# One scan over two states in a selective-scan kernel, its first step made apart

## The chip, the core and the metric

The kernel runs on one core of a Trainium2 chip. The metric is the device time of one execution in microseconds. The engines are named as in the profile: PE (TensorE, matmuls), DVE (VectorE), ACT (ScalarE), POOL (GpSimd) and SP (SyncE, which issues the DMAs). Each engine executes its own instructions in order, and waits where an instruction needs what another engine has not finished.

## What is computed

The input is 8192 rows of 512 numbers. A selective state-space block is followed by a quantized feed-forward block, each inside a layer norm, a modulation and a residual. The change concerns only the recurrence of the first block:

```
delta   = softplus(dlt @ W_dt.T + b_dt)              # [8192, 1024]
A       = -exp(A_log)                                # [1024, 16]
deltaA  = exp(delta[..., None] * A)                  # decay of each step
deltaBx = delta[..., None] * Bm[:, :, None, :] * xc[..., None]

def step(h, inp):                                    # over the 8192 steps
    dA, dBx, c = inp
    h = dA * h + dBx
    return h, einsum("bdn,bn->bd", h, c)
```

Each of the 1024 channels has 16 states `h`; a step multiplies each by its decay and adds an input, and the output of a channel is the sum of its states weighted by `c`.

## The kernel before

**Tiling.** The time axis is cut into 16 chunks of T = 512 steps, and the 1024 channels into ND = 8 blocks of 128, which lie on the partitions. Blocks are taken in NH = 4 parts `h` of DH = 2 blocks (`i`), and the 16 states in NG = 8 groups `g` of GN = 2. One *unit* is two states of one block over one chunk; `slot` numbers the units, 16 for each h and 64 for each chunk, 1024 in all. `where` gives k, h, g, i of a slot.

**One unit** (`unit`, L483) has these parts:

- `db` (L461, POOL) is the input of both states, a tile of 128 x 2 x 512, made two units ahead from the broadcast rows of B and from `du` (L355, POOL), which is delta times xc. There are three `db` buffers.
- `da` (L471, ACT) is the decay, `Exp(delta * na)`, one activation for each of the two states, made one unit ahead. It lies in PSUM, and there are two buffers.
- Two scans (L497, DVE), one for each state, run `h = da * h + db` along the 512 steps. Each starts from a column of `state`, in which the last step of the chunk before was kept.
- The last step of both states is put into `state` (the carry).
- The states are multiplied by the rows of C. PE then transposes the product and adds it up over the states in PSUM (`add_up`, L475, through `add_y`, L388).

Units come in two kinds. In 6 of each 16 (`FAR`, L440) the scan writes into an SBUF tile `hp`, and POOL makes the carry (L512) and the product with C (L513). These are the *far* units. In the other ten, the *near* units, the scan writes over `da`, and DVE makes the product (L521). The carry of a near unit is made by ACT at the beginning of the next unit if that one is far (L494), and by DVE otherwise (L520).

**Order.** The order of each engine's instructions is that of the program text; no planner moves them. Four moments of each unit (BEGIN, MID, GAP, END) are places for the work of other chunks: the norm of the rows, the convolution, the projections, `prep` (delta for one h), `du`, the gate and the output. `TABLE` (L533) gives for each step of each piece the place where it runs, as four times the unit, counted from the chunk's first, plus the moment. `LATER` (L441) gives in the same quarters how long after its unit each product is added up by PE.

`prep` (L343) is two Softplus activations, for the two blocks of one h. [...] a table is loaded before it (L347) and before the next Exp (L471).

`x_proj_out` (L325) copies the projection that holds dlt, B and C for a chunk from PSUM into `dbc` and writes B and C to memory, from which `load_bc` reads them back as broadcast rows.

Of the kernel before, what the change touches and what calls it, by code (L numbers as in the profile page):

```python
# [8 lines left out]
F32 = mybir.dt.float32  # L9
# [7 lines left out]
P = 128  # L17
# [81 lines left out]
def mamba_then_fp4_ffn(  # L99
# [27 lines left out]
    T = 512  # L127
# [16 lines left out]
    nc.gpsimd.memset(eps, EPS)  # L144
    slope0 = glob.tile([P, 1], F32, tag="slope0", name="slope0")
    nc.gpsimd.memset(slope0, -1.72)
    sc = glob.tile([P, NK], F32, tag="silu_c", name="silu_c")

    mo = [dram.tile([T, DM], F32, tag=f"mo_{k}", name=f"mo_{k}") for k in range(NC)]
# [8 lines left out]
    with ExitStack() as ma:  # L158
# [166 lines left out]
        def x_proj_out(k, _=None):  # L325
            pb = pend.pop(("pb", k))
            dbc = s1.tile([RK + 2 * NS, T], F32, tag="dbc", name=f"dbc_{k}")
            nc.scalar.activation(dbc, pb[: RK + 2 * NS, :], AF.Copy)
            bc = scr.tile([2 * NS, T], F32, tag="bc", name=f"bc_{k}")
            nc.sync.dma_start(bc, dbc[RK:, :])  # L330
            dbcs[k], bcd[k] = dbc, bc


        def prep_mm(k, h):
# [8 lines left out]
        def prep(k, h):  # L343
            delta = s2.tile([P, DH, T], F32, tag="delta", name=f"delta_{k}_{h}")
            for i in range(DH):
                d = h * DH + i
                nc.scalar.activation(  # L347
                    delta[:, i, :], pend.pop(("pd", k, d)), AF.Softplus, bias=bdt[:, d : d + 1]
                )
            deltas[k, h] = delta  # L350

        def make_du(k, d):
            h, i = divmod(d, DH)
            du = pools["du"].tile([P, T], F32, tag="du", name=f"du_{k}_{h}_{i}")
            nc.gpsimd.tensor_tensor(du, deltas[k, h][:, i, :], xcs[k, h * DH + i], ALU.mult)  # L355
            dus[k, h, i] = du

        def z_mm(k, m):
# [79 lines left out]


        FAR = (1, 3, 5, 9, 11, 13)  # L440
        LATER = (7, 7, 5, 10, 5, 16, 6, 3, 11, 8, 8, 8, 7, 9, 3, 3)  # L441

        def where(slot):
            k, r = divmod(slot, SLOT_C)
# [13 lines left out]
        def make_db(slot):  # L458
            k, h, g, i = where(slot)
            db = pools["db"].tile([P, GN, T], F32, tag="db", name=f"db_{slot}")  # L460
            nc.gpsimd.tensor_tensor(  # L461
                db, bct[slot // DH, 0], dus[k, h, i].unsqueeze(1).to_broadcast([P, GN, T]), ALU.mult
            )
            pend["db", slot] = db

        def make_da(slot, q):
            k, h, g, i = where(slot)
            d, n = h * DH + i, g * GN + q
            if q == 0:
                pend["da", slot] = pools["da"].tile([P, GN, T], F32, tag="da", name=f"da_{slot}")  # L470
            nc.scalar.activation(  # L471
                pend["da", slot][:, q, :], deltas[k, h][:, i, :], AF.Exp, scale=na[:, d, n : n + 1]
            )
# [9 lines left out]
        def unit(slot):  # L483
            k, h, g, i = where(slot)
            d = h * DH + i

            r = slot % SLOT_S
            far = r in FAR
            db = pend.pop(("db", slot))

            da = hs = pend.pop(("da", slot))
            to = pools["h"].tile([P, GN, T], F32, tag="hp", name=f"hp_{slot}") if far else hs
            if ("carry", slot - 1) in pend:
                nc.scalar.activation(*pend.pop(("carry", slot - 1)), AF.Copy)  # L494
            for q in range(GN):
                n = g * GN + q
                nc.vector.tensor_tensor_scan(  # L497
                    to[:, q, :], da[:, q, :], db[:, q, :], state[:, d, n : n + 1],
                    ALU.mult, ALU.add,
                )  # L500
            if slot + 1 < NSLOT:
                make_da(slot + 1, 0)
            carry = state[:, d, g * GN : (g + 1) * GN]
            run(slot, MID)
            if slot + 1 < NSLOT:
                make_da(slot + 1, 1)
            run(slot, GAP)
            if slot + 2 < NSLOT:
                make_db(slot + 2)
            c_rows = bct[slot // DH, 1]  # L510
            if far:
                nc.gpsimd.tensor_copy(carry, to[:, :, T - 1])  # L512
                nc.gpsimd.tensor_tensor(to, to, c_rows, ALU.mult)  # L513
                add = slot, to
            else:
                hc = pools["h"].tile([P, GN, T], F32, tag="hc", name=f"hc_{slot}")
                if r + 1 in FAR:
                    pend["carry", slot] = carry, hs[:, :, T - 1]
                else:
                    nc.vector.tensor_copy(carry, hs[:, :, T - 1])  # L520
                nc.vector.tensor_tensor(hc, hs, c_rows, ALU.mult)  # L521
                add = slot, hc
            if LATER[r] < 4:
                add_up(*add)
            else:
                at(slot + LATER[r] // 4, LATER[r] % 4, add_up, *add)
            if i == DH - 1:
                del bct[slot // DH, 0], bct[slot // DH, 1]
            run(slot, END)
# [2 lines left out]

        TABLE = {  # L533
            "norm": (
                (-323, -306, -300, -300, -297, -296, -292),
                (-307, -293, -293, -291, -289, -287, -281),
                (-305, -287, -280, -278, -277, -271, -266),
                (-290, -270, -266, -265, -262, -260, -253),
            ),
            "conv": (  # L540
                (-252, -246, -246, -243, -237, -234), (-229, -223, -219, -217, -211, -209),
                (-200, -194, -194, -188, -182, -179), (-171, -166, -166, -162, -156, -154),
                (-143, -137, -134, -133, -127, -126), (-120, -114, -114, -107, -104, -100),
                (-90, -88, -82, -78, -70, -69), (-60, -58, -56, -53, -47, -45),
            ),
            "x_proj": (
                (-36, -34, -31),
            ),
            "prep": (
                (-23, -17), (52, 54), (106, 112), (162, 164),  # L550
            ),
            "du": (
                (-15,), (-10,), (57,), (60,), (119,), (125,), (173,), (190,),
            ),
            "z": (
                (-14, -8, -4), (0, 6, 7), (59, 66, 66), (88, 98, 98), (152, 157, 160),
                (172, 174, 174), (176, 180, 183), (185, 191, 194),
            ),
            "skip": (
                (9, 17), (24, 30), (89, 94), (102, 120), (150, 152), (159, 182), (206, 210),  # L560
                (222, 228),
            ),
            "gate": (
                (67,), (67,), (134,), (134,), (195,), (196,), (259,), (262,),
            ),
            "gate_t": (
                (68, 77), (79, 87), (136, 142), (145, 150), (197, 203), (209, 215), (264, 270),
                (271, 275),
            ),
            "out": (  # L570
                (277, 277, 286), (288, 298, 304), (358, 359, 361), (370, 385, 389),
            ),
        }
        steps = {
            "norm": (load_x, norm_sum, norm_var, norm_rstd, norm_x, norm_t, norm_out),
            "conv": (conv_mm, conv_raw, conv_diag, conv_taps, conv_act, conv_out),
            "x_proj": (x_proj_0, x_proj_1, x_proj_out),
            "prep": (prep_mm, prep),
            "du": (make_du,),
            "z": (z_mm, z_act, z_out),  # L580
            "skip": (skip_act, skip),
# [4 lines left out]
        for k in range(NC):  # L586
            for name, fns in steps.items():
                if k == 0 and name in ("norm", "conv", "x_proj"):
                    continue
                for m, times in enumerate(TABLE[name]):  # L590
                    for fn, time in zip(fns, times):
                        if k == 1 and name == "norm":
                            time -= 4 * (6 if m > 1 else 4)
                        if k == 0 and name == "du" and time < 0:
                            time = min(time, 4 * -3 + GAP)
                        slot, moment = divmod(time, 4)
                        at(k * SLOT_C + slot, moment, fn, k, m)
# [5 lines left out]
        with tc.tile_pool(name="modp", bufs=1, side="right") as mp, tc.tile_pool(  # L603
# [140 lines left out]
            def neg_a():  # L744

                nc.vector.tensor_scalar(cw, cw, 0.5, None, ALU.mult)
                nc.scalar.activation(na, na, AF.Exp)
                nc.vector.tensor_scalar(na, na, -1.0, None, ALU.mult)

            load_x(0, 0)  # L750
            load_wm(0)
# [53 lines left out]
            on(20, x_proj, 0, 0)  # L805
            on(29, x_proj, 0, 1)
            on(29, x_proj_out, 0)
            for n, idx in enumerate((2, 5, 3, 4)):
                h = 8 + 6 * n
                for b in range(2):  # L810
                    on(h - 5 + 3 * b, mod_fetch, idx, b)
                    on(h - 3 + 3 * b, mod_mm, idx, b)
                if idx in (3, 4):
                    on(h + 1, mod_row, idx)
# [209 lines left out]
```

## Time and profile before

| | |
|---|---|
| Median of 3 runs | 5993.54 us (5990.07 to 5995.64) |
| Profiled execution, its own time | 5987.67 us |
| Its span | 5985.9 us |
| DVE busy in the span | 4924.4 us (82%) |
| POOL busy | 4141.6 us (69%) |
| ACT busy | 3080.0 us (51%) |
| PE busy | 5356.8 us (89%) |
| First scan to last scan starts | 157.7 to 3860.5 us |

The span runs from the first to the last instruction of the profiled execution. A busy share over the whole span is a mean over two stages, the scan stage up to about 3860 us and the feed-forward stage after it, in which DVE and POOL are less busy. In the lines of a group the part ahead of the bar is the line of the kernel, the engine, the operation, output and inputs by the program's names, the shapes and the count; after the bar are busy microseconds, the mean nanoseconds of one, and the idle time of the engine just before them with what ended most of it.

### The profile page before, as it was taken

The numbers are of one execution on the slowest core, as the hardware profiler recorded it, in microseconds if no ns is written. First come the engines' busy times: TensorE is split into PE (matmuls) and PEld (weight loads), VectorE is DVE, ScalarE is ACT, GpSimd is POOL, SyncE is SP. The second block draws the span as 40 slices with busy tenths as digits, with TensorE's granted clock in tenths as the row PEclk, the third lists the DMA queues.
The fourth block names the chain that finished last, engine by engine and source line by source line (L and its number), as shares of the span: only waits on it lengthen the run. The fifth ranks groups of instructions, "written<-read, shape, count | busy, mean of one in ns | idle before, by whom it ended". The sixth has DMA issues, their size and how long they took to land.

```text
span 5985.9 us, 60300 instructions
## 1 busy us (share of the span) xinstructions
PE 5356.8 (89%) x20772; PEld 3200.9 (53%) x20772; DVE 4924.4 (82%) x5007; ACT 3080.0 (51%) x5708; POOL 4141.6 (69%) x2415
## 2 busy tenths in 40 slices
PE   7788888889889889889888897679999999999999
PEld 4555565566555555555655655534444444444444
DVE  7999999999999999999999999875666666666654
ACT  6676676766776676766766665422222222222222
POOL 4999999999999999999999999732222222222221
PEclk9989999999999999999999998789999999999999
DMA  5444444444444444444444444410000000000000
GB/s 179 158 151 158 148 155 155 155 153 157 153 155 152 155 156 157 157 154 153 153 156 155 154 151 156 165 37 27 27 23 25 27 27 25 24 26 27 27 23 13
DMA packets 220553, 659.79 MB, mean 110 GB/s; under 512 B 24371, under 2 KB 36787, under 8 KB 220246
## 3 DMA queue, kind: packets, MB, share of 16 engines
q1 hardware_dynamic: 220246, 655.94, 33.7%
q8 instruction: 163, 2.67, 0.2%
q14 instruction: 144, 1.18, 0.1%
HBM read 615.48 MB, written 40.38 MB: 110 GB/s over the span
## 4 chain that ended last, share of the span: by engine, by line
PE 42%; DVE 23%; POOL 17%; ACT 10%; issue 8%; DMA 0%; DVEq 0%; POOLq 0%; SPq 0%; ACTq 0%
DVE da L497 12%; PE pg L945 10%; PE po L962 10%; POOL db L461 10%; PE pu L945 10%; ACT da L471 4%; POOL hp L513 4%; DVE hc L521 3%; DVE hp L497 3%; PE po L423 3%; PE y L392 2%; PE cv L268 2%; PE pz L366 2%; PE pt L913 2%; PE cv L296 1%
## 5 line engine op out<-in xcount | busy, mean ns | idle before, releaser
L461 POOL TENSOR_TENSOR db<-bc,du 128x1024 f32<-128x1024 f32 x1024 | 2395.0, 2361 | 38.2 <-DVE da L497 32.0
L497 DVE TENSOR_TENSOR_SCAN da<-da,state,db 128x512 f32<-128x512 f32 x1280 | 1645.3, 1285 | 85.7 <-ACT da L471 38.6
L471 ACT ACTIVATE da<-delta,na 128x512 f32<-128x512 f32 x2048 | 1407.7, 689 | 428.9 <-DVE hc L521 296.6
L87 POOL TENSOR_TENSOR hq<-xn,sc 128x1408 f32<-128x1408 f32 x64 | 189.2, 2956 | 1319.2 <-DVE xn L82 1319.2
L497 DVE TENSOR_TENSOR_SCAN hp<-da,state,db 128x512 f32<-128x512 f32 x768 | 941.0, 1267 | 44.9 <-ACT state L494 25.5
L392 PE MATMUL y<-ident,hc 128*128 128x128 f32 x5120 | 738.2, 294 | 224.4 <-DVE hc L521 183.6
L513 POOL TENSOR_TENSOR hp<-hp,bc 128x1024 f32<-128x1024 f32 x384 | 905.4, 2358 | 30.7
L392 PEld LDWEIGHTS y<-ident,hc 128*128 128x128 f32 x5120 | 633.3, 151 | 397.4 <-DVE hc L521 245.8
L521 DVE TENSOR_TENSOR hc<-da,bc 128x1024 f32<-128x1024 f32 x640 | 781.6, 1221 | 26.5 <-PE y L392 1.3
L945 PE MATMUL pg<-wg,xqT 128*128 128x512 f32 (+1 forms) x1536 | 653.5, 569 | 44.0 <-ACT xqT L937 44.0
L945 PE MATMUL pu<-wu,xqT 128*128 128x512 f32 (+1 forms) x1536 | 635.9, 557 | 0.0
L962 PE MATMUL po<-wd,hqT 128*128 128x512 f32 x1408 | 616.6, 594 | 0.0
L950 ACT ACTIVATE g<-pg 128x512 f32<-128x512 f32 (+1 forms) x192 | 107.8, 561 | 958.2 <-PE pg L945 958.2
L366 PE MATMUL pz<-w_in,hT 128*128 128x256 f32 x2048 | 483.1, 390 | 33.9 <-DVE z L381 29.1
L268 PE MATMUL cv<-hT,w_in 128*128 128x512 f32 x1024 | 476.9, 609 | 30.3 <-ACT delta L347 14.8
L945 PEld LDWEIGHTS pg<-wg,xqT 128*128 128x128 f32 x1536 | 290.6, 193 | 361.9 <-issue 251.0
L423 PE MATMUL po<-w_o,xc 128*128 128x512 f32 x1024 | 462.0, 600 | 20.3 <-DVE z L381 12.2
L296 PE MATMUL cv<-raw,taps 128*128 128x512 f32 x1024 | 469.0, 601 | 12.5 <-ACT taps L282 12.5
L951 DVE TENSOR_TENSOR h<-g,pu 128x512 f32<-128x512 f32 (+1 forms) x192 | 123.4, 643 | 427.0 <-PE pu L945 422.0
L392 PE MATMUL y<-ident,hp 128*128 128x128 f32 x3072 | 449.0, 295 | 26.9 <-POOL hp L513 26.9
L945 PEld LDWEIGHTS pu<-wu,xqT 128*128 128x128 f32 x1536 | 291.8, 190 | 313.3 <-issue 245.0
L392 PEld LDWEIGHTS y<-ident,hp 128*128 128x128 f32 x3072 | 393.4, 153 | 112.8 <-issue 50.0
(118 smaller groups left out, 6332.2 us busy)
## 6 DMA issues: line engine op xcount, KB each, us to landing
bc<-bc SPq DMA_DIRECT2D x1024, 512.0 KB, 4.5
x<-in_x_dram SPq DMA_DIRECT2D x64, 256.0 KB, 4.7
mo<-po SPq DMA_DIRECT2D x64, 256.0 KB, 2.1
h<-in_x_dram SPq DMA_DIRECT2D x64, 256.0 KB, 2.6
x<-mo SPq DMA_DIRECT2D x64, 256.0 KB, 2.6
out_dram<-x SPq DMA_DIRECT2D x64, 256.0 KB, 2.0
w_in<-in_w_inT_dram SPq DMA_DIRECT2D x2, 2048.0 KB, 9.2
wm<-in_wmod_dram SPq DMA_DIRECT2D x8, 512.0 KB, 4.6
```

The costliest lines, as they stand in the source:

```text
L268: nc.tensor.matmul(ps, lhsT=w_in[:, f, o : o + P], rhs=hT[k][:, f, :], start=(f == 0), stop=(f == NK - 1),)
L296: nc.tensor.matmul(v, lhsT=taps[:, i, :], rhs=raw[:, i : i + T], start=(i == 0), stop=(i == 3))
L366: nc.tensor.matmul(pz[:, b, :], lhsT=hT[k][:, f, t0 : t0 + P], rhs=w_in[:, f, o : o + DH * P], start=(b == 0 and f == 0), stop=(f == NK - ...
L392: nc.tensor.matmul(y[:, j, i * P : (i + 1) * P], lhsT=src[:, j * P : (j + 1) * P], rhs=ident, start=start and j % 2 == 0, stop=stop, is_tr ...
L423: nc.tensor.matmul(pend["po", k, j], lhsT=xcs[k, d][:, j * P : (j + 1) * P], rhs=w_o[:, d, :], start=(d == 0), stop=(d == ND - 1),)
L461: nc.gpsimd.tensor_tensor(db, bct[slot // DH, 0], dus[k, h, i].unsqueeze(1).to_broadcast([P, GN, T]), ALU.mult)
L471: nc.scalar.activation(pend["da", slot][:, q, :], deltas[k, h][:, i, :], AF.Exp, scale=na[:, d, n : n + 1])
L497: nc.vector.tensor_tensor_scan(to[:, q, :], da[:, q, :], db[:, q, :], state[:, d, n : n + 1], ALU.mult, ALU.add,)
L513: nc.gpsimd.tensor_tensor(to, to, c_rows, ALU.mult)
L521: nc.vector.tensor_tensor(hc, hs, c_rows, ALU.mult)
L945: nc.tensor.matmul(ps[:, :w], lhsT=qT[:, k, :], rhs=wt[:, k, o : o + w], start=(k == 0), stop=(k == NK - 1),)
L962: nc.tensor.matmul(po, lhsT=hT[:, f, :], rhs=wd[:, f, :], start=(f == 0), stop=(f == NF - 1))
```

## The change

The two scans of a unit become one scan over 1024 elements, that is, over the two rows of 512 one after the other. So that the second state does not go on from the end of the first, the decay of the first step of each row is made 0. Then the scan needs no start value, and what the first step must give, `exp(delta0 * A) * state + delta0 * B0 * x0`, is put into the first column of `db` instead.

- **Decay 0.** After delta of a block is made, its first column is overwritten with 1e30 (`huge`). `na` is at most -1e-28, so the exponent is -100 or less.
- **First step.** For each block `prep` has four more small activations on ACT: the decay of the first step for 16 states (`e0`), delta0 times xc0, that times B0 (`db0`), and the fill with `huge`. A new step `prep_add` multiplies `e0` by `state` and adds it to `db0`, two small operations on DVE for each block.
- **B0.** The 16 values of B of a chunk's first step are needed on all partitions: a small matmul into the PSUM tile of the projection (`first_mm`) and a copy by ACT (`first_out`), once a chunk.
- **Units.** `db` and `du` leave out their first column. Before the first `da` of each unit, ACT copies two columns of `db0` into the first column of each row of `db`. All near units leave their carry to ACT, so L520 goes.
- **Places.** `LATER` and `TABLE` have other numbers, and `x_proj` and `prep` have places for their new steps.

```diff
@@ x_proj_out and after it
-            dbcs[k], bcd[k] = dbc, bc
+            dbcs[k], bcd[k], pend["pb", k] = dbc, bc, pb
+
+        def first_mm(k, _=None):
+            nc.tensor.matmul(
+                pend["pb", k][:, :NS], lhsT=dbcs[k][:, 0:1].to_broadcast([RK + 2 * NS, P]),
+                rhs=ident[: RK + 2 * NS, RK : RK + NS], start=True, stop=True,
+            )
+
+        def first_out(k, _=None):
+            bf = small.tile([P, NS], F32, tag="bf", name=f"bf_{k}", bufs=1)
+            nc.scalar.activation(bf, pend.pop(("pb", k))[:, :NS], AF.Copy)
+            pend["bf", k] = bf
@@ prep
+                e0 = small.tile([P, NS], F32, tag="e0", name=f"e0_{k}_{d}", bufs=DH)
+                db0 = small.tile([P, NS], F32, tag="db0", name=f"db0_{k}_{d}")
+                pend["e0", k, d], pend["db0", k, d] = e0, db0
+            for i in range(DH):
+                d, d0 = h * DH + i, delta[:, i, 0:1]
+                nc.scalar.activation(pend["e0", k, d], na[:, d, :], AF.Exp, scale=d0)
+                nc.scalar.activation(d0, d0, AF.Copy, scale=xcs[k, d][:, 0:1])
+                nc.scalar.activation(pend["db0", k, d], pend["bf", k], AF.Copy, scale=d0)
+                nc.scalar.activation(d0, huge, AF.Copy)
             deltas[k, h] = delta
+
+        def prep_add(k, h):
+            for d in range(h * DH, (h + 1) * DH):
+                e0, db0 = pend.pop(("e0", k, d)), pend["db0", k, d]
+                nc.vector.tensor_tensor(e0, e0, state[:, d, :], ALU.mult)
+                nc.vector.tensor_tensor(db0, db0, e0, ALU.add)
@@ make_du
-            nc.gpsimd.tensor_tensor(du, deltas[k, h][:, i, :], xcs[k, h * DH + i], ALU.mult)
+            nc.gpsimd.tensor_tensor(
+                du[:, 1:], deltas[k, h][:, i, 1:], xcs[k, h * DH + i][:, 1:], ALU.mult
+            )
@@
-        LATER = (7, 7, 5, 10, 5, 16, 6, 3, 11, 8, 8, 8, 7, 9, 3, 3)
+        LATER = (7, 5, 7, 9, 6, 16, 6, 3, 10, 12, 7, 10, 7, 8, 4, 4)
@@ make_db
-                db, bct[slot // DH, 0], dus[k, h, i].unsqueeze(1).to_broadcast([P, GN, T]), ALU.mult
+                db[:, :, 1:], bct[slot // DH, 0][:, :, 1:],
+                dus[k, h, i][:, 1:].unsqueeze(1).to_broadcast([P, GN, T - 1]), ALU.mult,
@@ make_da, for the first state
+                first = pend["db0", k, d][:, g * GN : (g + 1) * GN]
+                nc.scalar.activation(pend["db", slot][:, :, 0], first, AF.Copy)
@@ unit
-            for q in range(GN):
-                n = g * GN + q
-                nc.vector.tensor_tensor_scan(
-                    to[:, q, :], da[:, q, :], db[:, q, :], state[:, d, n : n + 1],
-                    ALU.mult, ALU.add,
-                )
+            flat = lambda t: t.rearrange("p q t -> p (q t)")
+            nc.vector.tensor_tensor_scan(flat(to), flat(da), flat(db), 0.0, ALU.mult, ALU.add)
...
-                if r + 1 in FAR:
-                    pend["carry", slot] = carry, hs[:, :, T - 1]
-                else:
-                    nc.vector.tensor_copy(carry, hs[:, :, T - 1])
+                pend["carry", slot] = carry, hs[:, :, T - 1]
@@ TABLE: the rows that the text refers to (norm and conv have small shifts)
             "x_proj": (
-                (-36, -34, -31),
+                (-36, -34, -30, -27, -25),
             ),
             "prep": (
-                (-23, -17), (52, 54), (106, 112), (162, 164),
+                (-21, -18, -5), (54, 54, 59), (110, 112, 114), (161, 163, 176),
             ),
             "du": (
-                (-15,), (-10,), (57,), (60,), (119,), (125,), (173,), (190,),
+                (-15,), (-4,), (55,), (61,), (118,), (124,), (164,), (182,),
             ),
@@ neg_a
-                nc.vector.tensor_scalar(na, na, -1.0, None, ALU.mult)
+                nc.vector.tensor_scalar(na, na, -1.0, -1e-28, ALU.mult, ALU.min)
```

## The prediction

> **What bounds the kernel now.** I read the page's strip of busy tenths first: it falls into a scan stage and a feed-forward stage, and the edit touches only the first. Then the busy times over that stage, from the first scan to the last:
>
> ```profile
> core 0: us, PE busy (x) PEld busy (x) DVE busy (x) ACT busy (x) POOL busy (x), PEclk, DMA share, GB/s
> 155.60:3860.50 3704.90, 3227.00 (x14820) 2153.84 (x14821) 3530.59 (x3316) 2470.29 (x4773) 3522.66 (x1974) 0.94 0.47 154
> ```
>
> Columns are stretch, length, then busy time of each engine. DVE and POOL are both busy for 95% of it, ACT for 67%. So DVE work may be cut, but POOL stands 182 us below the stage, and nothing here makes POOL shorter. Next the costliest groups:
>
> ```profile
> L461 POOL TENSOR_TENSOR db<-bc,du 128x1024 f32<-128x1024 f32 x1024 | 2395.0, 2361 | 38.2 <-DVE da L497 32.0
> L497 DVE TENSOR_TENSOR_SCAN da<-da,state,db 128x512 f32<-128x512 f32 x1280 | 1645.3, 1285 | 85.7 <-ACT da L471 38.6 <-POOL state L512 16.3 <-POOL db L461 4.8
> L497 DVE TENSOR_TENSOR_SCAN hp<-da,state,db 128x512 f32<-128x512 f32 x768 | 941.0, 1267 | 44.9 <-ACT state L494 25.5 <-ACT da L471 19.4
> ```
>
> Two facts are in the idle columns: DVE's scans wait little (131 us in all), and part of that is for writes of `state` by POOL (L512) and ACT (L494), which concern columns that the waiting scan doesn't use. Then the DVE timeline, for the pace of a unit (start, duration):
>
> ```profile
> 2042.15 2.61 DVE L497 TENSOR_TENSOR_SCAN da<-da,state,db 128x512 f32<-128x512 f32 x2
> 2044.80 0.16 DVE L520 COPY state<-da 128x2 f32<-128x2 f32 x1
> 2044.87 1.21 DVE L521 TENSOR_TENSOR hc<-da,bc 128x1024 f32<-128x1024 f32 x1
> 2046.01 2.61 DVE L497 TENSOR_TENSOR_SCAN da<-da,state,db 128x512 f32<-128x512 f32 x2
> ...
> 2052.72 2.62 DVE L497 TENSOR_TENSOR_SCAN da<-da,state,db 128x512 f32<-128x512 f32 x2 [0.43 <-POOL state L512]
> 2055.43 1.23 DVE L521 TENSOR_TENSOR hc<-da,bc 128x1024 f32<-128x1024 f32 x1
> 2056.57 2.45 DVE L497 TENSOR_TENSOR_SCAN hp<-da,state,db 128x512 f32<-128x512 f32 x2
> 2058.94 0.66 DVE L306 SCALAR_TENSOR_TENSOR xc<-raw,cv 128x512 f32<-128x512 f32 x1
> ```
>
> A near unit takes 3.86 us from start to start with the carry copy and 3.85 without: that copy is already hidden. A far unit takes 2.37. A chunk has 40 near and 24 far units and 24 other DVE operations at 0.59 a step: 154.2 + 56.9 + 14.2 = 225.3 us. The pattern repeats every 232.1 us (L347's table load at 1419.63 and 1651.72), so DVE idles some 7 us a chunk. DVE sets the pace. Last, the hand-overs after `prep` of unit 13 (ACT) and around unit 60 (DVE, POOL):
>
> ```profile
> 1600.90 1.28 ACT L347 ACT_TABLE_LOAD   x1
> 1602.20 1.27 ACT L347 ACTIVATE delta<-pd,bdt 128x512 f32<-128x512 f32 x2
> 1603.48 1.28 ACT L471 ACT_TABLE_LOAD   x1
> 1604.78 2.75 ACT L471 ACTIVATE da<-delta,na 128x512 f32<-128x512 f32 x4
> ```
> ```profile
> 1606.29 2.62 DVE L497 TENSOR_TENSOR_SCAN da<-da,state,db 128x512 f32<-128x512 f32 x2 [0.85 <-ACT da L471]
> ```
> ```profile
> 1531.56 4.67 POOL L461 TENSOR_TENSOR db<-bc,du 128x1024 f32<-128x1024 f32 x2
> 1539.98 2.37 POOL L461 TENSOR_TENSOR db<-bc,du 128x1024 f32<-128x1024 f32 x1
> 1543.52 2.35 POOL L461 TENSOR_TENSOR db<-bc,du 128x1024 f32<-128x1024 f32 x1
> ```
> ```profile
> 1534.36 2.62 DVE L497 TENSOR_TENSOR_SCAN da<-da,state,db 128x512 f32<-128x512 f32 x2 [0.21 <-issue]
> 1542.38 2.62 DVE L497 TENSOR_TENSOR_SCAN da<-da,state,db 128x512 f32<-128x512 f32 x2 [0.26 <-POOL db L461]
> 1546.85 2.61 DVE L497 TENSOR_TENSOR_SCAN da<-da,state,db 128x512 f32<-128x512 f32 x2
> ```
>
> `prep` holds ACT for 3.88 us (1600.90 to 1604.78). The scan at 1606.29 starts only after the second half of its `da` (two times 0.72 after 1604.78), though its first half needs only the first. With the `state` waits this says that order is kept by whole tiles, not by columns. And POOL is hardly ahead: the scans at 1534.36, 1542.38 and 1546.85 start 0.5, 0.0 and 1.0 us after their `db` (ready at 1533.9, 1542.35, 1545.87).
>
> [...] L244 (one column, pointer scale) measures 291 and the table load 1283[...]. [...]
>
> **Part by part.**
> *The scan.* [...] Near unit 3.59, far 2.25: 40 and 24 of them are 197.6 us against 211.1. Saved: 13.5 us a chunk. [...]
> *`prep_add`.* [...] About 1.8 of it falls in stalls described below; 1.0 counts.
> *Carries.* L520 goes (worth nothing, see above); its 256 copies join ACT at L494's 168 ns, ahead of `da`. The waits of scans on `state` go too: about 42 us in the whole run.
> *ACT in every unit.* The first-column copy, like L289 (195 ns, 0.15 a step), comes before `da`. From the end of `hc` of unit s−1: 0.03, carry 0.20, copy 0.15, two `da` 1.42, hand-over 0.05: `da` of s+1 is ready 1.85 later. A far unit gives it 2.25 less the 0.09 by which scan and `hc` overlap: no stall, 0.3 to spare.
> *ACT in `prep`.* [...] `prep` grows from 3.88 to 5.98 us. Bounds: 1.6 to 2.9 more, −32 to +51 us over 64 `prep`.
> What that does: at unit 13 (far, starting at t), `da` of 14 is ready at t + 1.9, `prep` ends at 7.9, `da` of 15 at 9.5. DVE has done units 13 and 14 at 2.25 + 3.59 = 5.84. Stall: 3.7 us. The same sum with the present numbers gives 0.9, and 0.85 is measured. Walking ACT and DVE through the 64 units so, with the new table: 3.7 at 13, 3.7 at 28, 2.8 at 40, 4.5 at 59 (with a `norm_x` behind it), 2.2 in the dense norm steps of units 53 to 58, 0.5 elsewhere: 17.4.
> Sum for DVE and ACT: 197.6 + 14.2 + 1.0 + 17.4 = 230.2 us a chunk, 1.9 under today.
> *The new wait.* The copy writes a tile that POOL has just filled. If order is kept by tiles, it waits for POOL's `db`, and `da` is queued behind it: a scan then starts at least 1.65 us after its `db`. The trace has leads of 0.0, 0.5, 1.0. In a stretch where POOL never pauses this is one shift, not a loss for each unit; it becomes a loss where POOL waits for a far scan that is now later (L512, 110 us today). Not shown by the trace: nothing to 8 us a chunk; I take 2.8, a good half microsecond for each group of 16 units.
> *At nothing:* POOL's operations one column shorter; the fill of `huge`, `first_mm` and `first_out` (once a chunk); the limit on `na` (once). POOL's cover is the 5% that it idles.
> Sum: 233.0 − 232.1 = +0.9 us, by 16: **+14 us**. Against the profiled execution (5987.67, span 5985.9) that is 6002; the median shown is 5.9 higher, so **6008 us**.
>
> **The rivals.**
> A, faster: the copy doesn't wait for POOL, or POOL keeps its lead. For it: DVE's sum is certain to fall, and POOL catches up in each `prep` stall. Against: the leads above. 16 × (230.2 − 232.1) = −30, and −70 with a cheap scan or `prep`: about 5945. It decides while the copy's waits cost less than 1.1 us a chunk.
> B, faster still: ACT's stalls fall where DVE would wait for POOL anyway, and POOL alone is the bound: 3522.7/16 = 220.2, with 1% of waits 222.4 a chunk, −155: 5838. Against: a stall of 3.7 four times in a chunk exceeds what POOL is behind.
> C, clearly slower: POOL, ACT and DVE in series, at the full 8 us: +100: 6095. It decides from 1.9 us of added waits a chunk.
> D, slower: `db` on rows of 511 from an odd element. POOL operations of 1024 columns differ by pattern (L69 2310, L87 2007 ns); at +300 ns POOL needs 239 a chunk: 6105. It decides from 0.15 us a `db`.
>
> **How the numbers follow.** Forecast 0.42, A 0.24, B 0.08, C 0.18, D 0.08. Its own range is 5975 to 6045. For eight in ten I take in A's and most of C's: 5915 to 6085. About 0.2% (12 us) can be told from no change. Of the forecast's 0.42, 0.05 is faster, 0.14 same and 0.23 slower; A gives 0.22 and 0.02; C and D are slower: faster 0.35, same 0.16, slower 0.49.
>
> **What would show it.** One scan of 128x1024 at 2.33 to 2.35 us; DVE's busy time down by some 170; ACT's up by about 380; DVE's wait for ACT's `da` up from 58 to over 200 us, in lumps near 3.5 at each `prep`; waits for `state` gone from the scans; the first-column copy waiting for POOL's `db`. It is wrong if the lumps are under 2 us (then A), if the copy never waits for POOL (A), if POOL is over 98% busy (B), or if `db` is longer than 2.4 us (D).

## The result, and the profile after

The changed kernel takes 6043.98 us (median of 6 runs, 6023.51 to 6054.97) against 5996.4 us of the kernel before (6 runs beside it). The ratio is 1.0076, 95% interval 1.0058 to 1.0093: slower by some 45 us. The profiled execution took 6043.94 us, its span is 6042.2 us.

Busy time of the engines over the scan stage of the kernel after, in the columns of the same view of before (stretch, length, PE, PEld, DVE, ACT, POOL):

```profile
155.60:3915.00 3759.40, 3258.77 (x14862) 2181.26 (x14863) 3459.31 (x2290) 2718.53 (x6587) 3517.38 (x1973) 0.93 0.47 152
```

DVE has 71 us less to do than before (3459 for 3531), ACT 248 more, POOL 5 less. DVE's idle time in the stage rose from 174 to 300 us (length less busy). So the change did take work from DVE, and more than that came back as waits. First scan to last scan starts 169.3 to 3918.6 us: the stage begins 11.6 us later, and is 46.5 us longer, 2.9 a chunk. Behind it lie 2123.6 us against 2125.4: nothing else changed.

The costliest groups of the page after (busy time and mean of one behind the bar, then idle time before and its releasers):

```profile
L494 POOL TENSOR_TENSOR db<-bc,du 128x1022 f32<-128x1022 f32 x1024 | 2392.8, 2357 | 30.2 <-DVE da L532 26.0
L532 DVE TENSOR_TENSOR_SCAN da<-da,db 128x1024 f32<-128x1024 f32 x640 | 1461.2, 2283 | 71.3 <-ACT da L507 53.8
...
L532 DVE TENSOR_TENSOR_SCAN hp<-da,db 128x1024 f32<-128x1024 f32 x384 | 875.3, 2279 | 89.9 <-ACT da L507 69.0
```

A flat scan takes 2283 and 2279 ns, 1461.2 + 875.3 = 2336.5 us in all against 2586.3 before: 250 us less, and the carry copies of L520, some 40 us, are gone too. But DVE's busy time fell by only 71. The missing 220 us are two groups that the kernel before hadn't got, from the list of DVE's groups:

```profile
L381 DVE TENSOR_TENSOR db<-db,e 128x16 f32<-128x16 f32 x128 | 170.4, 1331 | 11.0 <-ACT db L373 3.6
L380 DVE TENSOR_TENSOR e<-e,state 128x16 f32<-128x16 f32 x128 | 50.1, 391 | 33.7 <-ACT e L371 33.7
```

These are the two operations of `prep_add`, on 16 columns each. One takes 1331 ns on average, more than a product of 1024 columns (1221). Together they are busy for 220.5 us, 13.8 a chunk. The timelines of DVE and of POOL at one `prep_add` show why (start, duration):

```profile
1448.26 0.44 DVE L380 TENSOR_TENSOR e<-e,state 128x16 f32<-128x16 f32 x1 [0.99 <-ACT e L371]
1448.93 2.08 DVE L381 TENSOR_TENSOR db<-db,e 128x16 f32<-128x16 f32 x1 [0.23 <-ACT db L373]
1450.93 0.16 DVE L380 TENSOR_TENSOR e<-e,state 128x16 f32<-128x16 f32 x1
1451.20 1.06 DVE L381 TENSOR_TENSOR db<-db,e 128x16 f32<-128x16 f32 x1
```
```profile
1446.33 2.35 POOL L545 TENSOR_TENSOR hp<-hp,bc 128x1024 f32<-128x1024 f32 x1
1448.63 2.35 POOL L494 TENSOR_TENSOR db<-bc,du 128x1022 f32<-128x1022 f32 x1
1450.94 1.29 POOL L386 TENSOR_TENSOR du<-delta,xc 128x511 f32<-128x511 f32 x1
```

POOL's operations end at 1448.68, 1450.98 and 1452.23. The long DVE operations end at 1448.70, 1451.01 and 1452.26, each 0.02 to 0.03 us later; the only short one (0.16) starts where one POOL operation gives way to the next. The view of waits lists none for POOL at these two lines, only 33.7 and 3.6 us for ACT: the time is inside the instruction. The three long operations here last as long as the rest of what POOL is doing. This is not a choice of examples: of the 256 small operations of the run, 134 took over 300 ns, and every one of them ended 26 to 39 ns after the end of a POOL operation. (Beside POOL's one-column `rstd`, L240, 14 sums were not held: 174 to 176 ns.) The scan stage of the trace before couldn't warn of it. Its products of C (least, median and longest duration 1208/1224/1226 ns), its scans (1253 to 1294) and its convolution (628/672/690) were even throughout; each has one input in PSUM, and so has the gate. The line of the gate's product (the same three numbers), beside a POOL that is busy 95% of the time:

```profile
L404 DVE TENSOR_TENSOR z<-z,y x128: 658/677/687, 217.7 to 3865.8; 128x512 f32<-128x512 f32 x128
```

For L381 after, the same three numbers are 174, 1186 and 2334.

But the feed-forward stage of the trace before did show it. There L81 and L82 are operations of the same kind on the same 512 columns, both with two SBUF inputs, and L82 takes nearly four times as long. The groups of that trace with shapes kept apart, then DVE's and POOL's timeline at one L82:

```profile
L82 DVE SCALAR_TENSOR_TENSOR xn<-e,xn 128x512 f32<-128x512 f32 x66 | 173.5, 2629 | 2.1
L81 DVE SCALAR_TENSOR_TENSOR xn<-e,xn 128x512 f32<-128x512 f32 x66 | 46.9, 711 | 0.4
```
```profile
4524.18 2.96 DVE L82 SCALAR_TENSOR_TENSOR xn<-e,xn 128x512 f32<-128x512 f32 x1
```
```profile
4523.62 2.97 POOL L87 TENSOR_TENSOR hq<-xn,sc 128x1408 f32<-128x1408 f32 x1 [20.43 <-DVE xn L82]
```

L82 ends at 4527.14, 0.55 us after POOL's operation (4526.59). The same holds of all 57 of the 66 that began beside a running POOL operation (545 to 551 ns after its end); the other nine have a median of 691 ns. The distance from POOL's end thus grows with the columns: about 31 ns for 16, 548 for 512, which is some 1.04 ns a column (an estimate from these two medians). So these held operations seem to wait for POOL's end first and to do their own work then.

### The profile page after: what moved, and what is told of

Its sections match the earlier page's. It is cut to its first block, busy times and chain, and to the rows that moved or that the text cites. A ratio compares the mean times of both kernels' runs of the same rounds, so it can differ in the third digit from the quotient of the medians.

```text
span 6042.2 us, 61643 instructions
## 1 busy us (share of the span) xinstructions
PE 5383.5 (89%) x20804; PEld 3226.4 (53%) x20804; DVE 4858.7 (80%) x3983; ACT 3322.2 (55%) x7515; POOL 4136.9 (68%) x2416
## 5 line engine op out<-in xcount | busy, mean ns | idle before, releaser
L494 POOL TENSOR_TENSOR db<-bc,du 128x1022 f32<-128x1022 f32 x1024 | 2392.8, 2357 | 30.2 <-DVE da L532 26.0
L532 DVE TENSOR_TENSOR_SCAN da<-da,db 128x1024 f32<-128x1024 f32 x640 | 1461.2, 2283 | 71.3 <-ACT da L507 53.8
L532 DVE TENSOR_TENSOR_SCAN hp<-da,db 128x1024 f32<-128x1024 f32 x384 | 875.3, 2279 | 89.9 <-ACT da L507 69.0
L425 PE MATMUL y<-ident,hc 128*128 128x128 f32 x5120 | 725.5, 290 | 158.5 <-DVE hc L550 119.3
L550 DVE TENSOR_TENSOR hc<-da,bc 128x1024 f32<-128x1024 f32 x640 | 781.6, 1221 | 77.1 <-PE y L425 39.7
L399 PE MATMUL pz<-w_in,hT 128*128 128x256 f32 x2048 | 503.2, 402 | 39.9 <-ACT delta L361 20.5
L270 PE MATMUL cv<-hT,w_in 128*128 128x512 f32 x1024 | 491.6, 625 | 24.0 <-ACT hT L263 22.3
L298 PE MATMUL cv<-raw,taps 128*128 128x512 f32 x1024 | 481.2, 613 | 10.8 <-ACT taps L284 9.5
L399 PEld LDWEIGHTS pz<-w_in,hT 128*128 128x128 f32 x2048 | 407.1, 204 | 116.8 <-ACT delta L361 29.9
L530 ACT ACTIVATE state<-da 128x2 f32<-128x2 f32 x639 | 108.4, 170 | 649.9 <-DVE hc L550 649.1
```

Source lines behind the costliest of these rows:

```text
L270: nc.tensor.matmul(ps, lhsT=w_in[:, f, o : o + P], rhs=hT[k][:, f, :], start=(f == 0), stop=(f == NK - 1),)
L298: nc.tensor.matmul(v, lhsT=taps[:, i, :], rhs=raw[:, i : i + T], start=(i == 0), stop=(i == 3))
L399: nc.tensor.matmul(pz[:, b, :], lhsT=hT[k][:, f, t0 : t0 + P], rhs=w_in[:, f, o : o + DH * P], start=(b == 0 and f == 0), stop=(f == NK - ...
L425: nc.tensor.matmul(y[:, j, i * P : (i + 1) * P], lhsT=src[:, j * P : (j + 1) * P], rhs=ident, start=start and j % 2 == 0, stop=stop, is_tr ...
L494: nc.gpsimd.tensor_tensor(db[:, :, 1:], bct[slot // DH, 0][:, :, 1:], dus[k, h, i][:, 1:].unsqueeze(1).to_broadcast([P, GN, T - 1]), ALU.mult,
L532: nc.vector.tensor_tensor_scan(flat(to), flat(da), flat(db), 0.0, ALU.mult, ALU.add)
```

## The experiments

Ratios are to the kernel before, run beside each; "after" stands for the changed kernel.

**Without the additions, and with them on POOL.** Two edits of `prep_add`. The first moves both operations to the other engine, the second leaves them out, so the part of the first step that comes from `state` is missing.

```diff
-                nc.vector.tensor_tensor(e0, e0, state[:, d, :], ALU.mult)
-                nc.vector.tensor_tensor(db0, db0, e0, ALU.add)
+                nc.gpsimd.tensor_tensor(e0, e0, state[:, d, :], ALU.mult)
+                nc.gpsimd.tensor_tensor(db0, db0, e0, ALU.add)
```

> The two small adds of prep_add run on POOL in place of DVE. Theory T (a DVE operation with both inputs in SBUF is held until POOL's running operation ends, so that the two take 391 and 1331 ns [...]): DVE's 220 us for them go, POOL takes some 60 us more, and the time falls by 40 to 70 us from 6044, to about before (5985 to 6005). Rival R (the adds lie in the stall that ACT's longer prep makes anyway): within 10 us of 6044.

> prep_add is left out, so the state of the chunk before isn't carried over; everything else stays. Theory T: as with the adds on POOL or a little lower, 5965 to 6000, since POOL has nothing more to do. Rival R: within 10 us of 6044.

Left out: 5914.20 us, ratio 0.9878 (0.9864 to 0.9893), 50 us and more below what was expected. So the other parts of the change make the kernel faster by 1.2%, and the additions alone turn that into a loss. On POOL: 6005.76 us, 1.0031 (1.0020 to 1.0043), at the upper edge of what was expected: better than on DVE and not good. POOL's additions hold up ACT, whose first-column copy needs them (view of waits of that run: who, for whom, us in total, times, longest):

```profile
ACT db L505 <- POOL db L381: 54.4, 31, 3.2
```

The run without additions also shows the stalls after `prep` by themselves. DVE's timeline of one chunk, its scans that waited for ACT:

```profile
1404.15 2.29 DVE L530 TENSOR_TENSOR_SCAN hp<-da,db 128x1024 f32<-128x1024 f32 x1 [3.64 <-ACT state L528]
...
1448.78 2.30 DVE L530 TENSOR_TENSOR_SCAN da<-da,db 128x1024 f32<-128x1024 f32 x1 [2.49 <-ACT da L505]
...
1495.67 2.30 DVE L530 TENSOR_TENSOR_SCAN da<-da,db 128x1024 f32<-128x1024 f32 x1 [0.75 <-ACT da L505]
...
1515.72 2.29 DVE L530 TENSOR_TENSOR_SCAN hp<-da,db 128x1024 f32<-128x1024 f32 x1 [4.51 <-ACT da L505]
...
1579.73 2.30 DVE L530 TENSOR_TENSOR_SCAN da<-da,db 128x1024 f32<-128x1024 f32 x1 [2.31 <-ACT state L528]
```

3.64 + 2.49 + 0.75 + 4.51 + 2.31 = 13.7 us a chunk. Counted by units, the four large ones lie one behind each `prep`: those of units 28, 40 and 59, and that of unit 13 in the next chunk; the 0.75 is at unit 56. Two are listed under ACT's carry (L528), though the flat scan doesn't read `state` at all. ACT's timeline shows what that name is worth. The `da` of the scan at 1404.15 is made here:

```profile
1402.67 1.40 ACT L505 ACTIVATE da<-delta,na 128x512 f32<-128x512 f32 x2
```

It is ready at 1404.07, and the scan starts 0.08 us later. All 83 scans of this run that are listed as waiting for ACT, under either name, start 87 to 103 ns after their own `da`. The name under which a wait is listed needn't be the one that mattered: these are all waits for `da`, 124.7 + 97.5 = 222.2 us. The same holds of the kernel before: 77 of the 78 waits that are listed under `state` there ended 87 to 90 ns after the scan's own `da`.

**What is held: the operation's inputs, or its place.** The changed kernel with a maximum in place of the product, and a copy in place of the sum. The part from `state` is left out here too.

```diff
-                nc.vector.tensor_tensor(e0, e0, state[:, d, :], ALU.mult)
-                nc.vector.tensor_tensor(db0, db0, e0, ALU.add)
+                nc.vector.tensor_reduce(e0[:, 0:1], e0, AX.X, ALU.max)
+                nc.vector.tensor_copy(e0, db0)
```

> The changed kernel with other operations in place of the two additions of a block: a maximum over the 16 columns of e0 (one input in SBUF, output one column) for the product, and a copy of db0 into e0 for the sum. The first step then leaves out the part that comes from the state before. Theory (a VectorE operation with two SBUF inputs is held until GpSimd's running operation ends, one with a single SBUF input is not): the maximum takes under 300 ns on average with its longest under 500, and, if the copy isn't held either, the time is within 15 us of the kernel without the additions (5914). Rival (whatever stands at that place of VectorE is held for GpSimd): both kinds have means of about 400 to 1300 ns and the time stays at 6025 to 6055. Between them: the maximum free and the copy held, 5960 to 6000.

6021.47 us, ratio 1.0061 (1.0046 to 1.0076). DVE's groups of this run, then its timeline at one place and POOL's beside it:

```profile
L381 DVE COPY e<-db 128x16 f32<-128x16 f32 x128 | 174.3, 1362 | 16.4 <-ACT db L373 9.4
L380 DVE TENSOR_REDUCE e<-e 128x1 f32<-128x16 f32 x128 | 20.1, 157 | 34.3 <-ACT e L371 34.3
```
```profile
1436.68 0.17 DVE L380 TENSOR_REDUCE e<-e 128x1 f32<-128x16 f32 x1 [1.24 <-ACT e L371]
1437.34 2.08 DVE L381 COPY e<-db 128x16 f32<-128x16 f32 x1 [0.50 <-ACT db L373]
1439.34 0.16 DVE L380 TENSOR_REDUCE e<-e 128x1 f32<-128x16 f32 x1
1439.60 1.04 DVE L381 COPY e<-db 128x16 f32<-128x16 f32 x1
```
```profile
1434.74 2.35 POOL L545 TENSOR_TENSOR hp<-hp,bc 128x1024 f32<-128x1024 f32 x1
1437.05 2.35 POOL L494 TENSOR_TENSOR db<-bc,du 128x1022 f32<-128x1022 f32 x1
1439.35 1.26 POOL L386 TENSOR_TENSOR du<-delta,xc 128x511 f32<-128x511 f32 x1
```

The maximum at 1436.68 starts and ends in the middle of POOL's operation (1434.74 to 1437.09): it isn't held. The longest of its 128 took 171 ns. The copy from SBUF to SBUF is held to the end of POOL's operation twice (1439.40 and 1440.61), as the sum was. So the place isn't what counts, and "two SBUF inputs" is not all: a plain copy pays too, 1362 ns on average. The rival that everything at this place is held falls. My time for the mixed outcome (5960 to 6000) was too low: it took the two operations as sharing the cost evenly, but the held copy takes up nearly the whole of it (174.3 us against 170.4), and only the 30 us between 50.1 and 20.1 could be won. The run also answers two other rivals. In the changed kernel ACT's first-column copy waits 32.1 us for the sum; here nothing waits for the copy that took its place, and 107 of the 130 us between the kernels with and without additions are still lost. And DVE's own waits for ACT at these two operations aren't the loss: they are 37 us in the changed kernel, 44 here, and 56 in the kernel with paired additions at the same places (below), which is 70 us faster than the changed kernel.

**Fewer operations, and another place.** If a held operation costs the rest of one POOL operation whatever its size, two operations for both blocks of an h should cost half of four. The second of these runs has only that; the first also puts `prep_add` straight behind `prep`.

```diff
-            for d in range(h * DH, (h + 1) * DH):
-                e0, db0 = pend.pop(("e0", k, d)), pend["db0", k, d]
-                nc.vector.tensor_tensor(e0, e0, state[:, d, :], ALU.mult)
-                nc.vector.tensor_tensor(db0, db0, e0, ALU.add)
+            e0, db0 = pend.pop(("both", k, h))
+            nc.vector.tensor_tensor(e0, e0, state[:, h * DH : (h + 1) * DH, :], ALU.mult)
+            nc.vector.tensor_tensor(db0, db0, e0, ALU.add)
@@ the first run only
-                (-21, -18, -5), (54, 54, 59), (110, 112, 114), (161, 163, 176),
+                (-21, -18, -13), (54, 54, 59), (110, 112, 115), (161, 163, 167),
```

> The adds of both blocks of one h in two DVE operations of 32 columns in place of four of 16, and put directly behind prep in all four places, where DVE waits for ACT anyway. Theory T (each add is held by POOL's running operation, whatever its size): half the held time, most of it in the stall: 5930 to 5970, below before. Rival (the cost is in the work or the waits, not in the count): 6000 or more.

> The changed kernel with the additions of both blocks of an h in one product and one sum of 32 columns, at the changed kernel's own places. Theory (a held operation costs what is left of GpSimd's operation, whatever its size, so the count decides): busy time of the additions 110 to 150 us in place of 220, time 5950 to 5990. Rival (it was the earlier place directly behind prep that gained in the run with paired additions): 6010 to 6045.

At the old places: 5973.27 us, ratio 0.9976 (0.9969 to 0.9983); straight behind `prep`: 5931.90 us, 0.9906 (0.9891 to 0.9920). Both are as expected, and both beat the kernel before. DVE's groups of the faster one:

```profile
L383 DVE TENSOR_TENSOR db<-db,e 128x32 f32<-128x32 f32 x64 | 72.9, 1140 | 13.0 <-ACT db L376 8.2
L382 DVE TENSOR_TENSOR e<-e,state 128x32 f32<-128x32 f32 x64 | 63.5, 992 | 53.9 <-ACT e L374 52.8
```

Twice the columns, and the sum's mean is no longer than that of 16 columns. 136.4 us are left of 220.5 (143.5 at the old places), so the count brings some 80 us of busy time and 60 us of time (1.0076 to 0.9976). The place brings another 42 (to 0.9906). In the changed kernel two of the four `prep_add` lie some 6 us after the stall that their `prep` caused, so DVE pays for both. Here are those stalls with their additions in the changed kernel's DVE timeline, and then the same units in the faster run:

```profile
1497.88 2.30 DVE L532 TENSOR_TENSOR_SCAN da<-da,db 128x1024 f32<-128x1024 f32 x1 [2.49 <-ACT da L507]
...
1504.52 2.33 DVE L381 TENSOR_TENSOR db<-db,e 128x16 f32<-128x16 f32 x1
...
1570.86 2.29 DVE L532 TENSOR_TENSOR_SCAN hp<-da,db 128x1024 f32<-128x1024 f32 x1 [4.67 <-ACT da L507]
1576.97 1.21 DVE L380 TENSOR_TENSOR e<-e,state 128x16 f32<-128x16 f32 x1
1578.21 1.19 DVE L381 TENSOR_TENSOR db<-db,e 128x16 f32<-128x16 f32 x1
```
```profile
1457.36 0.85 DVE L382 TENSOR_TENSOR e<-e,state 128x32 f32<-128x32 f32 x1 [0.17 <-ACT e L374]
1458.31 0.19 DVE L383 TENSOR_TENSOR db<-db,e 128x32 f32<-128x32 f32 x1
1459.79 2.30 DVE L534 TENSOR_TENSOR_SCAN da<-da,db 128x1024 f32<-128x1024 f32 x1 [1.28 <-ACT da L509]
...
1528.39 1.16 DVE L382 TENSOR_TENSOR e<-e,state 128x32 f32<-128x32 f32 x1 [1.29 <-ACT e L374]
1529.66 2.21 DVE L383 TENSOR_TENSOR db<-db,e 128x32 f32<-128x32 f32 x1
```

The additions now lie within the wait for `da`: DVE's waits for it fall from 122.8 to 45.1 us (8.8 more are listed under the carry), while those for `e0` at the additions rise from 33.7 to 52.8.

**Two variants of that kernel.**

```diff
@@ the one
-        LATER = (7, 5, 7, 9, 6, 16, 6, 3, 10, 12, 7, 10, 7, 8, 4, 4)
+        LATER = (7, 7, 5, 10, 5, 16, 6, 3, 11, 8, 8, 8, 7, 9, 3, 3)
@@ the other
-            nc.vector.tensor_tensor(e0, e0, state[:, h * DH : (h + 1) * DH, :], ALU.mult)
-            nc.vector.tensor_tensor(db0, db0, e0, ALU.add)
+            nc.gpsimd.tensor_tensor(e0, e0, state[:, h * DH : (h + 1) * DH, :], ALU.mult)
+            nc.gpsimd.tensor_tensor(db0, db0, e0, ALU.add)
```

> The kernel with paired additions behind prep, with the LATER numbers of the kernel before. If the new LATER numbers are worth nothing of themselves: 5925 to 5940, within 0.15% of the paired kernel. If they were needed for the faster units (TensorE adding up too early for POOL's far products or too late for the buffers): 5950 to 6010.

> The paired additions behind prep, on POOL in place of DVE. POOL is not held by itself, but waits for ACT's prep and ACT's next first-column copy waits for POOL, as in the run with single additions on POOL (6006). Theory: POOL's waiting for prep costs more than DVE's being held, so slower than the paired kernel on DVE: 5960 to 6000. Rival (only the holding cost anything): 5890 to 5920.

With the old `LATER`: 5946.93 us, 0.9936 (0.9921 to 0.9951), between the two expectations. The intervals of 0.9906 and 0.9936 just fail to meet, so the new numbers are worth a little, some 0.3%. The other new places of `TABLE` were not tried by themselves. On POOL: 5998.04 us, 1.0020 (1.0012 to 1.0029), as expected of the theory. The additions are short on POOL (32 columns took it 242 to 267 ns), but scans wait 221 us for `da` (130 under that name, 91 under the carry's), as they do without additions, ACT's copy waits 32.5 us for POOL's sum, and in the scan stage DVE waits 69 us for ACT's `z`, against 8 without additions. Here being held, inside a stall that is there anyway, was cheaper than another hand-over between engines.

**The small activations spread out.** The four small activations of a block are moved from `prep` to two later near units, the additions straight behind them, once on DVE and once on POOL. This was meant to break up the stalls.

```diff
-                (-21, -18, -5), (54, 54, 59), (110, 112, 114), (161, 163, 176),
+                (-21, -18, -14, -13, -6, -5), (54, 54, 58, 59, 62, 63),
+                (110, 112, 114, 115, 122, 123), (161, 163, 170, 171, 178, 179),
...
-            "prep": (prep_mm, prep, prep_add),
+            "prep": (prep_mm, prep, first_0, add_0, first_1, add_1),
```

> The four small activations of each block are taken out of prep and put into two later near units, where ACT has 1.6 us to spare, and the adds, still on DVE, right after them. Theory A (the 2.1 us that they add to prep are paid in full by DVE's wait for da): that wait falls from 123 to under 75 us, but the held adds now lie on DVE's path with nothing beside them, so the time moves by -70 to +10 us from 6044. Rival (prep's length is hidden): the wait for da stays over 110 us.

> Both edits together. Theories T and A: the two costs are gone, the time falls by 90 to 150 us from 6044, to 5895 to 5955, below before. Rival P (POOL alone is the bound by then): POOL over 97% busy in the scan stage and the time at 5960 or more.

6135.68 us, 1.0250 (1.0234 to 1.0265), and on POOL 6090.64 us, 1.0173 (1.0158 to 1.0189): both much slower, and both outside their expectations, the second by far. POOL isn't the bound that its rival named: it is busy 3560 of 3792 us of the scan stage (94%). The waits of DVE in the first:

```profile
DVE e L386 <- ACT e L373: 119.0, 48, 12.0
...
DVE da L544 <- ACT da L519: 31.1, 31, 1.5
```

The waits for `da` did fall, from 122.8 to 31 us. But DVE now meets ACT's small activations in the middle of a unit and waits for them, 119 us for 34, and the additions, still held (283 us busy), have no stall to lie in.

**One part alone in the kernel before.** First only the flat scan (no start value, so the second state runs on from the first and no chunk carries in); then only four small activations for each block in `prep`, into tiles that nothing reads.

```diff
-            for q in range(GN):
-                n = g * GN + q
-                nc.vector.tensor_tensor_scan(
-                    to[:, q, :], da[:, q, :], db[:, q, :], state[:, d, n : n + 1],
-                    ALU.mult, ALU.add,
-                )
+            flat = lambda t: t.rearrange("p q t -> p (q t)")
+            nc.vector.tensor_tensor_scan(flat(to), flat(da), flat(db), 0.0, ALU.mult, ALU.add)
@@ the other run: in prep, after both Softplus
+            for i in range(DH):
+                d = h * DH + i
...
+                nc.scalar.activation(e0, na[:, d, :], AF.Exp, scale=delta[:, i, 0:1])
+                nc.scalar.activation(d1, delta[:, i, 0:1], AF.Copy, scale=xcs[k, d][:, 0:1])
+                nc.scalar.activation(db0, e0, AF.Copy, scale=d1)
+                nc.scalar.activation(d1, eps, AF.Copy)
```

> The kernel before with one scan over both states and nothing else of the change, so the second state goes on from the end of the first and no state is carried. This is the gain by itself. Theory: DVE's sum falls from 225.3 to 211.5 us a chunk and POOL's 220 becomes the bound, with 1 to 2% of waits: 130 to 165 us under before, 5820 to 5860. Rival (POOL already sets the pace, the gain is hardly there to be given back): 5940 or more.

> The kernel before with the four small activations of each block added in prep, into tiles that nothing reads, and nothing else. Theory A (2.1 us of ACT in each of 64 prep are paid in full by DVE, 0.4 us of slack apart): 100 to 140 us over before, 6085 to 6125. Rival (ACT, busy for two thirds, hides them): within 20 us of before.

The flat scan alone: 5960.66 us, 0.9954 (0.9937 to 0.9970). The scans are as fast as in the changed kernel (2290 and 2282 ns), and yet only some 28 us come out of 244. The expectation (5820 to 5860) was missed, and the time is the rival's. The rest became waits of DVE, here from that run's list:

```profile
DVE da L496 <- ACT da L471: 156.1, 140, 3.0
DVE hp L496 <- ACT state L494: 65.1, 48, 2.5
DVE da L496 <- POOL db L461: 48.6, 65, 1.6
DVE hc L517 <- PE y L392: 31.3, 14, 3.3
```

Before, they were 38.6, 25.5, 4.8 and 1.3. (The waits under `state` end 86 to 102 ns after the scan's own `da` here too.) With the places as they were, ACT and POOL don't deliver faster than DVE used to ask. The small activations alone: 6113.11 us, 1.0210 (1.0195 to 1.0226). In the old kernel a longer `prep` costs 125 us, as expected.

**Is it still `prep` without the additions?** The changed kernel without the additions and without three of the four small activations; only the fill is kept, and the first step is left out.

```diff
-                nc.scalar.activation(pend["e0", k, d], na[:, d, :], AF.Exp, scale=d0)
-                nc.scalar.activation(d0, d0, AF.Copy, scale=xcs[k, d][:, 0:1])
-                nc.scalar.activation(pend["db0", k, d], pend["bf", k], AF.Copy, scale=d0)
                 nc.scalar.activation(d0, huge, AF.Copy)
```

> The changed kernel without prep_add and with only the fill left of the four small activations; the first step's result is taken from a tile of zeros, so it is left out. To be held against the run without the adds (5914). Theory A: 1.6 us less in each prep, 60 to 100 us under 5914, down to 5815 to 5855, where POOL's sum stops it. Rival: within 20 us of 5914.

5940.65 us, 0.9923 (0.9908 to 0.9938): the expectation was missed by 85 us and more, and it is even slower than with all four (0.9878). What the theory said of `da` came true: with those listed under the carry, DVE's waits for it fell from 222.2 to 158.3 us (124.3 + 34.0). But others grew by more: those of the products with `z`, for ACT and PE, from 59.2 to 118.4 us, and those for POOL's `db` from 9.9 to 39.6. POOL is busy 3512 us of the 3653 from first to last scan (96%). So once the additions are gone, a shorter `prep` only moves the waits to other places. Which order of which engine keeps these two kernels at 5914 and 5941 isn't settled; that POOL stands at 96 to 97% there speaks for POOL being close to its limit, but no run here cut POOL's work.

## Why the prediction was right, step by step

The time lies 36 us above the forecast, within its own range and on its side. It is right as a sum of terms that were off both ways, and that these nearly cancelled was luck. Most of the signs that the prediction named did not come: the scan took 2.28 us and not 2.33, DVE's busy time in the stage fell by 71 us and not by 170, ACT's rose by 248 and not by 380, and the first-column copy never waited for POOL, which the prediction itself had named as a sign of being wrong. A chunk's account, from the stage's length (first to last scan, by 16) and from the run without additions:

| a chunk, us | forecast | measured |
|---|---|---|
| scans and products | 197.6 | 193.7 (worked out: at the forecast's 2.35 and 2.33 us the scans are 2398.7 us, measured 2336.5, so 62 less in all) |
| other DVE work | 14.2 | 14.2 (not measured again) |
| stalls for ACT | 17.4 | 13.7 (run without additions) |
| waits for PE's `y` | none | 4.7 (run without additions, 75.8 us) |
| sum of these | 229.2 | 226.3; that run's stage is 226.0 |
| `prep_add` | 1.0 | 8.3 (234.3 − 226.0) |
| copy waits for `db` | 2.8 | none |
| sum | 233.0 | 234.3, before 231.4 |

- **The scan** was forecast at 2.33 to 2.35 us and took 2.28. The forecast rested on what 512 more elements add, which no trace had shown: the kernel before has scans of 512 alone (1285 and 1267 ns). They add 998 and 1012 ns, less than a scan of 512; whether the constant start or something else makes the difference, no run shows; nor does one try the copy L520 by itself. The waits listed under `state` fell from 42 to 1.4 us, but this bears nothing out: they were waits for `da` all along (see the run without additions, where 97.5 us stand under that name).
- **`prep_add`** is the term that was clearly mis-sized. It was forecast at 1.8 us a chunk inside the stalls and 1.0 beside them, from a duration that no trace of before had shown for 16 columns, and measured 13.8 us, of which 8.3 shows in the time. The shortest sum took 174 ns, but their median was 1186. This is the step of the prediction that failed. It took a duration for granted without asking what POOL, busy 95% of the time, was doing at that moment.
- **`prep` and its stalls.** `prep` holds ACT for 6.1 us, 5.98 were forecast. (From the trace of before I would estimate 6.0: for each block three operations like L244, 291 ns, and one like L289, 195, so 2.14 more than 3.88.) The stalls behind unit 40 and 59 are 2.49 and 4.67 (forecast 2.8 and 4.5), in the run without additions the one behind 28 is 3.64 (3.7), and the one behind 13 is 2.31 (3.7; the scan of unit 13 itself waits another 1.31 us there, for PE's `y`). The forecast of over 200 us of DVE waiting for `da` wasn't met as written (122.8). In the run without additions it is 222.2, listed in two parts: ACT's lateness is as large as forecast, and in the changed kernel the additions fill a part of it.
- **The new wait** was wrong. The first-column copy never waits for POOL's `db`; ACT's longest wait there is for the additions:

```profile
ACT db L505 <- DVE db L381: 32.1, 16, 2.5
```

  That POOL was always done in time isn't the reason: 20 scans did wait for `db` (8.3 us), with their copy and `da` already made. Here order is thus kept by columns, and the argument from whole tiles did not carry over to `db`. Half of it was a misreading: the waits under `state`, which seemed to concern columns that the scan doesn't use, were waits for `da`. For `da` it holds in the trace before.
- **Not foreseen:** the waits for PE's `y` (18 us by far scans and 40 by products after, 1.3 before), and the later start of the stage, 11.6 us, which the forecast had left out (8.6 us of it are there without the additions too).
- **The rivals.** D is out: `db` from an odd element takes 2357 ns against 2361. C is out with its wait. A's condition, that the copy doesn't wait, held, and without the additions the time fell by 1.2%, further than A's 5945. B's bound is near in the kernels without additions, with POOL at 96 to 97% of the stage, but not in the changed one (3513 of 3749 us, 94%). It was thus the held additions, which neither the forecast nor a rival had, that put the result on the slow side.

The best kernel of the study is the one with paired additions straight behind `prep`: 5931.90 us, 0.9906 of the time before.

## What to carry to other kernels

In the changed kernel, with GpSimd busy 94% of the scan stage, a VectorE operation of 16 columns was not small with both its inputs in SBUF (391 and 1331 ns on average), nor, in one run, as a copy from SBUF to SBUF (1362). In a kernel like it, cost such an operation at what is left of GpSimd's running operation plus its own elements (its end came a median of 31 ns after GpSimd's with 16 columns, 548 with 512), make few of them (220.5 us for 256, 136.4 for 128), and put them where VectorE waits anyway (another 42 us of time). Look for it in the spread of durations (shortest, median, longest) and in ends that agree with the other engine's ends, since no wait showed it here. And a saving on the busiest engine was only as large as the lead of those that feed it: 244 us less of scans brought 28 us while the order around them stayed. Last, before a wait is explained by the name under which it is listed, compare the start of what waited with the ends of all that it needed: here over 40 us before, and 97 in one run, stood under the wrong name.

## What the runs showed of the hardware that was not expected

- VectorE operations of 16 columns took 146 to 2377 ns with two SBUF inputs beside GpSimd, the end being GpSimd's end plus 26 to 39 ns in all of the 134 that took over 300 ns. 32 columns took 191 to 2328 ns (means 992 and 1140), and 57 operations of 512 columns in the kernel before ended 545 to 551 ns after GpSimd's end. A maximum over 16 columns with one SBUF input took 142 to 171 ns in the same place; a copy SBUF to SBUF took 180 to 2349. GpSimd's own operations were not lengthened (2357 ns against 2361).
- A scan over 1024 elements with a constant start took 2283 ns, against 1285 for 512 with a start from memory, twice of which is 2570.
